# Context keys for two batches at once, first tokens by tiles and new ranks in a planned cross-attention kernel

## The chip, the cores and the metric

The kernel runs on one core of a Trainium2 chip. That core has TensorE (matrix products; PE, with PEld for its weight loads), VectorE (DVE), ScalarE (ACT), GpSimd (POOL) and SyncE (SP, here only a queue that issues DMAs). The metric is the device time of one launch in microseconds (us), as the median of several runs. The profiler records one execution; its span goes from the first to the last instruction.

## The reference, cut to what matters

Two layers over 16 batches of 256 tokens with 256 features, and a context of 77 tokens a batch. All data is float32.

```python
# layer 0
h = rmsnorm(x, sa_norm_w);   h = x + attention(h, h, sa_wq, sa_wk, sa_wv, sa_wo)    # 16 heads of 16
hn = rmsnorm(h, ca_norm_w);  h = h + attention(hn, context, ca_wq, ca_wk, ca_wv, ca_wo)
hn = rmsnorm(h, mlp_norm_w); h = h + (silu(hn @ w_gate) * (hn @ w_up)) @ w_down      # 1024 wide
# layer 1, with layer 0's output as queries and the context as features
norm_X, norm_F = layernorm(context), layernorm(h)
attended = softmax(norm_F @ norm_X.T / 16) @ norm_X                                  # one head of 256
cross = gelu(attended @ fc1_w.T + fc1_b) @ fc2_w.T + fc2_b                           # through 4 features
n = layernorm(cross);  own = softmax(n @ n.T / 16) @ n
out = norm_F + gamma2 * (cross + gamma1 * own)
```

`attention` takes scores of each head times 1/4, a softmax over the keys, the weighted values and the output matrix. The context enters layer 0 through `ca_wk` and `ca_wv`, which don't depend on the tokens.

## The kernel before

**Work.** The program takes the batches one by one in layer 0, and in pairs (`UB = 2`) for loading tokens, for storing them and for layer 1 (the last pair in layer 1 batch by batch). Each piece of the work is a Python generator, called a stream. For a batch there are `self_operands` (norm, transposes psq, psk, psv), `self_maxima` (scores `sc`, row maxima by VectorE), `exponentials` (scores again, transposed, as `st`, exponentials by ScalarE into `pT`), `outputs` (`po`, values with a column of ones), `projection` (division and `wo`); the same for the context with a leading `c` (`csc`, `cst`, `cpo`, `cwo`), fed by `cross_queries` (`pscq`) and `cross_keys`; then `mlp` (`pg`, `pu`, `wd`). For a pair there are `second_context` and `second`, which are layer 1.

**Heads.** A head has 16 features, so score products use 32 rows of TensorE at a time and value products 32 columns. A step of the program has a shape: `f` (full array), `r` (row groups) or `c` (column groups). All score products share one set of four PSUM banks (`sc_banks`); one product must be read out before the next can start.

**Context keys.** `cross_keys(b)` transposes the 77 context tokens of a batch (`tpc`, copied to `ctxT`), multiplies them by `cwk` (`psck`), writes the masked keys `ckm` with ScalarE and the keys with ones `ckx` with VectorE, then makes the values (`pscv`, copied into `cvone`). `ckm` and `ckx` have two buffers, one batch each. `load_context` loads one batch ahead of that, into `cx`.

**Order.** Four engines (TensorE, ScalarE, VectorE, GpSimd) run in an order that a planner in the program writes out (class `Order`). Every stream yields steps with a duration, the data it needs, buffers it acquires and releases, and what it gives. At each turn the planner takes the first TensorE step by this key:

```python
wait = 20 if "f" in (self.shape, st.step.shape) else 500
late = t > self.clock["P"] + wait
key = (late, t if late else 0, st.rank)
```

A step counts as late if it could start only more than `wait` ns after TensorE is free; among those not late the lowest rank goes first. Ranks are given with `add(rank, tie, stream)`: about the batch number plus a constant for the stage, from -50 for the context's exponentials to 4 for the MLP, which so fills what is left. SyncE isn't planned by itself: its DMAs go out in the order in which the program writes them, and the queue waits at each for its buffer.

**Start.** SyncE issues the first pair of tokens as one load of 512 KB, then two contexts, the next pair of tokens and the matrices from `cwk` on; ScalarE issues `wq` to `wo`; GpSimd issues three norm weights, makes the identity, and sets constants: `vone` (three buffers of 1024 columns with ones, into which the values are copied), `cvone`, `nmax`. GpSimd also computes the power -1/2 of every norm (`rstd`, line 193).

Of the kernel before, what the change touches and what calls it, by code (L numbers as in the profile page):

```python
# [15 lines left out]
P = 128  # L16
# [13 lines left out]
def kernel(  # L30
# [46 lines left out]
    def tokens(ap, u):  # L77
# [4 lines left out]
        "h": 4, "cx": 2, "cx2": 2, "hn": 3, "hnT_sa": 1, "hnT_ca": 1, "hnT_mlp": 1, "ctxT": 1,  # L82
        "qx": 3, "kx": 3, "vone": 3, "cqT": 2, "cqx": 2, "ckm": 2, "ckx": 2, "cvone": 2, "pT": 2,
        "po": 1,
        "os": 1, "cos": 1, "oq": 1, "coq": 1, "oT": 1, "coT": 1, "sg": 2, "gT": 1,
# [3 lines left out]
    def load_tokens(u):  # L89
        hs[u] = hpool.tile([P, NT, D], F32, tag="h", name=f"h{u}", bufs=BUFS["h"])  # L90
        nc.sync.dma_start(hs[u], tokens(x, u))
# [6 lines left out]
    load_tokens(0)  # L98
    for b in range(2):
        cxs[b] = load_context(b, 1, "cx")  # L100
# [31 lines left out]
    ca_nw = load_columns(ca_norm_w, "ca_nw", nc.gpsimd)  # L132
# [4 lines left out]
    mlp_nw = load_columns(mlp_norm_w, "mlp_nw", nc.gpsimd)  # L137
# [5 lines left out]
    ident = const.tile([P, P], F32, tag="ident", name="ident")  # L143
    make_identity(nc, ident)
# [17 lines left out]

    vones, cvones, maxes = [], [], ([], [])
    for i in range(3):
        t = const.tile([P, QT, NH, 2 * HD], F32, tag=f"vone{i}", name=f"vone{i}")
        nc.gpsimd.memset(t, 1.0)
        vones.append(t)
# [65 lines left out]
    class Order:  # L233
# [72 lines left out]
        def run(self):  # L306
            while self.streams:
                best = None
                aux = []
                for st in self.streams:  # L310
# [3 lines left out]
                    if st.step.pe:  # L314

                        wait = 20 if "f" in (self.shape, st.step.shape) else 500
# [109 lines left out]
    class Attention:  # L426
# [14 lines left out]
        def tile(self, tag, shape, n=""):  # L441
            tag = self.name + tag
            return pool.tile(shape, F32, tag=tag, name=f"{tag}{self.b}_{n}", bufs=BUFS[tag])
# [615 lines left out]
    def context_loads():  # L1059
        for b in range(B):  # L1060
# [3 lines left out]
            if b > 1:  # L1064
                cxs[b] = load_context(b, 1, "cx")
# [76 lines left out]
```

## Time and profile before

| | us |
|---|---|
| median of 3 runs | 1022.9 |
| lowest and highest run | 1022.3, 1024.54 |
| the profiled execution | 1023.16 |
| its span | 1021.4 |
| TensorE busy | 973.7 |
| VectorE busy | 592.5 |
| ScalarE busy | 512.3 |
| GpSimd busy | 85.0 |

The mean granted clock of TensorE is 0.987. The execution's own time is 1.8 us longer than its span: what lies before the first and after the last recorded instruction. Busy times of engines overlap. In a row of the timeline the first number is when the instruction started, the second how long it took; matmul ends are modelled, so distances between starts are the safer measure. Every float32 product shows as two instructions.

### The profile page before, as it was taken

The page shows a single profiled execution, that of the slowest core. Times are in us where ns is not written, and L with a number is a line of the kernel's source. Part 1 is how long each engine was busy: PE and PEld are TensorE (multiplying, and loading weights), DVE is VectorE, ACT ScalarE, POOL GpSimd, SP SyncE. Part 2 cuts the span into 40 slices and gives each one's busy share as a digit, 9 for nine tenths or more (in the row PEclk, how much of TensorE's full clock was granted, in tenths as well). Part 3 has the DMA queues.
Part 4 walks back from the last instruction along what each step waited for, and adds up shares of the span by engine and source line. Part 5 has one row for each costly group of instructions (what it writes and reads, how often), then busy time and mean ns, then how long its engine had stood idle before and what let it go on. Part 6 is the DMA issues. An engine that isn't in the chain of part 4 may idle for free.

```text
span 1021.4 us, 18993 instructions
## 1 busy us (share of the span) xinstructions
PE 973.7 (95%) x8179; PEld 709.6 (69%) x8179; DVE 592.5 (58%) x1032; ACT 512.3 (50%) x900; POOL 85.0 (8%) x122
## 2 busy tenths in 40 slices
PE   5888999999999999999999999999999999999995
PEld 4655666767776777768676786767777677776772
DVE  2866475757565667465674665655764655455542
ACT  3555736443756347363663526555274537343532
POOL 3100000000100001000110001000010002001110
PEclk9999999999999999999999999999999999999995
DMA  9100000000001000000001000010000000000000
GB/s 300 24 9 1 4 1 2 2 1 1 4 8 46 1 1 1 31 25 1 1 7 49 2 1 1 11 46 1 1 1 10 25 2 1 21 1 1 1 22 21
DMA packets 16908, 17.58 MB, mean 17 GB/s; under 512 B 2392, under 2 KB 16312, under 8 KB 16824
## 3 DMA queue, kind: packets, MB, share of 16 engines
q1 hardware_dynamic: 15640, 15.32, 4.7%
q8 instruction: 64, 1.05, 0.4%
q10 hardware_dynamic: 1088, 1.05, 0.3%
q0 software_dynamic: 96, 0.00, 0.1%
q14 instruction: 20, 0.16, 0.1%
HBM read 12.13 MB, written 4.19 MB: 16 GB/s over the span
## 4 chain that ended last, share of the span: by engine, by line
PE 84%; DVE 6%; ACT 5%; DMA 3%; issue 1%; POOL 0%; POOLq 0%; ACTq 0%
PE wd L728 11%; PE pg L699 11%; PE pu L699 10%; PE st L525 7%; PE sc L473 6%; PE po L556 5%; PE cpo L556 3%; PE cst L525 3%; PE psq L399 3%; PE cwo L594 3%; PE pscq L399 3%; PE wo L594 3%; PE psk L399 3%; ACT pT L533 2%; PE psv L626 2%; DMA h<-in_x_dram 2%
## 5 line engine op out<-in xcount | busy, mean ns | idle before, releaser
L533 ACT ACTIVATE pT<-st 128x2048 f32<-128x2048 f32 x64 | 120.4, 1881 | 83.2 <-PE st L525 83.0
L478 DVE TENSOR_REDUCE nmax<-sc 128x8 f32<-128x2048 f32 x64 | 146.4, 2287 | 19.4 <-PE sc L473 18.2
L699 PE MATMUL pg<-hnT_mlp,wg 128*128 128x256 f32 x512 | 129.1, 387 | 0.0
L728 PE MATMUL wd<-wd,gT 128*128 128x256 f32 x512 | 127.5, 388 | 0.0
L699 PE MATMUL pu<-hnT_mlp,wu 128*128 128x256 f32 x512 | 126.9, 385 | 0.5 <-DVE sg L710 0.5
L699 PEld LDWEIGHTS pg<-hnT_mlp,wg 128*128 128x128 f32 x512 | 93.2, 190 | 23.6 <-issue 13.0
L699 PEld LDWEIGHTS pu<-hnT_mlp,wu 128*128 128x128 f32 x512 | 93.4, 190 | 19.0 <-issue 7.4
L728 PEld LDWEIGHTS wd<-wd,gT 128*128 128x128 f32 x512 | 91.9, 190 | 20.5 <-issue 10.0
L710 DVE SCALAR_TENSOR_TENSOR sg<-sg,pg 128x512 f32<-128x512 f32 x64 | 44.0, 688 | 75.3 <-ACT sg L709 75.0
L709 ACT ACTIVATE sg<-pg 128x512 f32<-128x512 f32 x64 | 38.0, 594 | 65.4 <-PE pg L699 65.0
L533 ACT ACTIVATE cpT<-cst 77x2048 f32<-77x2048 f32 x32 | 59.9, 1873 | 19.1 <-PE cst L525 18.8
L556 PE MATMUL po<-pT,vone 128*32 128x256 f32 x1024 | 66.7, 384 | 0.0
L503 DVE TENSOR_REDUCE nmax<-csc 128x16 f32<-128x1232 f32 x32 | 46.1, 1441 | 29.9 <-PE csc L496 29.8
L711 DVE SCALAR_TENSOR_TENSOR gT<-sg,pu 128x512 f32<-128x512 f32 x64 | 43.8, 685 | 25.0 <-PE pu L699 24.1
L556 PEld LDWEIGHTS po<-pT,vone 128*32 128x32 f32 x1024 | 27.6, 109 | 29.2 <-issue 16.0
L193 POOL TENSOR_TENSOR rstd_n<-ve_n,neg_half 128x4 f32<-128x4 f32 (+2 forms) x26 | 22.3, 864 | 248.7 <-DVE ve_n L191 131.7
L399 PE MATMUL pscq<-hnT_ca,cwq 128*128 128x256 f32 x128 | 31.6, 390 | 3.8 <-ACT hnT_ca L359 3.8
L399 PE MATMUL psq<-hnT_sa,wq 128*128 128x256 f32 x128 | 34.3, 407 | 0.6 <-ACT hnT_sa L359 0.6
L556 PE MATMUL cpo<-cpT,cvone 77*32 77x256 f32 x512 | 34.3, 385 | 0.1
L399 PE MATMUL psk<-hnT_sa,wk 128*128 128x256 f32 x128 | 33.9, 397 | 0.0
L626 PE MATMUL psv<-wv,hnT_sa 128*128 128x256 f32 x128 | 31.9, 386 | 0.0
L399 PEld LDWEIGHTS pscq<-hnT_ca,cwq 128*128 128x128 f32 x128 | 23.1, 190 | 10.6 <-ACT hnT_ca L359 4.3
(619 smaller groups left out, 1568.2 us busy)
## 6 DMA issues: line engine op xcount, KB each, us to landing
h<-in_x_dram SPq DMA_DIRECT2D x8, 512.0 KB
out_dram<-h SPq DMA_DIRECT2D x7, 512.0 KB
cx<-in_ctx_dram SPq DMA_DIRECT2D x16, 77.0 KB
cx<-in_ctx_dram SPq DMA_DIRECT2D x8, 154.0 KB
wg<-in_L_xattn_w_gate_dram SPq DMA_DIRECT2D x1, 1024.0 KB
wu<-in_L_xattn_w_up_dram SPq DMA_DIRECT2D x1, 1024.0 KB
wd<-in_L_xattn_w_down_dram SPq DMA_DIRECT2D x1, 1024.0 KB
out_dram<-h SPq DMA_DIRECT2D x2, 256.0 KB
```

The costliest lines, as they stand in the source:

```text
L399: nc.tensor.matmul(ps[:, m * n : (m + 1) * n], lhsT=w[:, c, m * P : (m + 1) * P], rhs=srcT[:, c, :], start=(c == 0), stop=(c == NC - 1),)
L473: nc.tensor.matmul(sc[:, j, (1 - e) * S : (2 - e) * S], lhsT=a.qx[rg, c, e, qt * P : (qt + 1) * P], rhs=a.kx[rg, c, e], start=True, stop=True,
L478: nc.vector.tensor_reduce(maxima_of(nm, qt)[:, :, c::NC], sc.rearrange("p j (y k) -> p j y k", y=2), AX.X, ALU.max, negate=True,)
L503: nc.vector.tensor_reduce(maxima_of(nm, qt), sc[:, :, : 2 * NC * SK].rearrange("p j (n k) -> p j n k", k=SK), AX.X, ALU.max, negate=True,)
L525: nc.tensor.matmul(st[:nk, j, e * S : (e + 1) * S], lhsT=a.kx[rg, c, e, kc * P : kc * P + nk], rhs=a.qx[rg, c, e], start=True, stop=True,)
L533: nc.scalar.activation(a.pT[k][:nk].rearrange("p j e q -> p j (e q)"), st[:nk], AF.Exp, scale=HD ** -0.5,)
L556: nc.tensor.matmul(po[RG * j : RG * (j + 1), e, :], lhsT=a.v[:nk, kc, 8 * c + 2 * j + e, :], rhs=pT[:nk, j, e, :], start=(first and e == 0 ...
L594: nc.tensor.matmul(ps[:, i * D : (i + 1) * D], lhsT=oT[:, c, i * P : (i + 1) * P], rhs=a.w[:, c, :], start=(c == 0), stop=(c == NC - 1),)
L626: nc.tensor.matmul(ps[:, t * D : (t + 1) * D], lhsT=hnT[:, c, t * P : (t + 1) * P], rhs=wv[:, c, :], start=(c == 0), stop=(c == NC - 1),)
L699: nc.tensor.matmul(ps[:, i * S : (i + 1) * S], lhsT=w[:, c, (f + i) * P : (f + i + 1) * P], rhs=hnT[:, c, :], start=(c == 0), stop=(c == N ...
L710: nc.vector.scalar_tensor_tensor(sg, sg, 1.0, ps, ALU.add, ALU.mult)
L728: nc.tensor.matmul(ps[:, :D], lhsT=gT[:, f, i * P : (i + 1) * P], rhs=wd[:, f, :], start=(f == 0), stop=(f == NF - 1),)
```

## The change

- `cross_keys` takes a pair of batches: four transposes into one bank, one copy to `ctxT` (154 columns), one `psck` of 154 columns, one `ckm` and one `ckx` for both; values still by batch. `ckm`, `ckx` and `cx` have one buffer, which holds a pair. They are released by the pair's last batch. Contexts are loaded by pairs.
- The first pair of tokens is loaded as four tiles of 128 tokens, with the first pair of contexts after two of them.
- The `vone` memsets move from GpSimd to VectorE; the identity is made first on GpSimd; `ca_nw` and `mlp_nw` are loaded from SyncE's queue.
- `os`, `oq` and `oT` are shared by self and cross attention; `os` has two buffers.
- `wait` between row and column steps is 100 ns in place of 500. `cross_maxima` needs the batch before it (`cmT`, b - 1) in place of the one before that.
- Ranks come from a table with a constant for every stage, one added for the first two batches and one for the last three.
- Planned time to landing of context loads is 4000 ns in place of 3000.

```diff
-        "h": 4, "cx": 2, "cx2": 2, "hn": 3, "hnT_sa": 1, "hnT_ca": 1, "hnT_mlp": 1, "ctxT": 1,
-        "qx": 3, "kx": 3, "vone": 3, "cqT": 2, "cqx": 2, "ckm": 2, "ckx": 2, "cvone": 2, "pT": 2,
+        "h": 4, "cx": 1, "cx2": 2, "hn": 3, "hnT_sa": 1, "hnT_ca": 1, "hnT_mlp": 1, "ctxT": 1,
+        "qx": 3, "kx": 3, "vone": 3, "cqT": 2, "cqx": 2, "ckm": 1, "ckx": 1, "cvone": 2, "pT": 2,
         "po": 1,
-        "os": 1, "cos": 1, "oq": 1, "coq": 1, "oT": 1, "coT": 1, "sg": 2, "gT": 1,
+        "os": 2, "oq": 1, "oT": 1, "sg": 2, "gT": 1,
...
-    def load_tokens(u):
-        hs[u] = hpool.tile([P, NT, D], F32, tag="h", name=f"h{u}", bufs=BUFS["h"])
-        nc.sync.dma_start(hs[u], tokens(x, u))
+    def load_tokens(u, t=None):
+
+        if not t:
+            hs[u] = hpool.tile([P, NT, D], F32, tag="h", name=f"h{u}", bufs=BUFS["h"])
+        part = slice(NT) if t is None else slice(t, t + 1)
+        nc.sync.dma_start(hs[u][:, part], tokens(x, u)[:, part])
...
-    load_tokens(0)
-    for b in range(2):
-        cxs[b] = load_context(b, 1, "cx")
+    for t in range(NT):
+        if t == QT:
+            cxs[0] = load_context(0, UB, "cx")
+        load_tokens(0, t)
...
+    ident = const.tile([P, P], F32, tag="ident", name="ident")
+    make_identity(nc, ident)
     sa_nw = load_columns(sa_norm_w, "sa_nw", nc.gpsimd)
+
+    vones, cvones, maxes = [], [], ([], [])
+    for i in range(3):
+        t = const.tile([P, QT, NH, 2 * HD], F32, tag=f"vone{i}", name=f"vone{i}")
+        nc.vector.memset(t, 1.0)
+        vones.append(t)
...
-    ca_nw = load_columns(ca_norm_w, "ca_nw", nc.gpsimd)
+    ca_nw = load_columns(ca_norm_w, "ca_nw", nc.sync)
...
-    mlp_nw = load_columns(mlp_norm_w, "mlp_nw", nc.gpsimd)
+    mlp_nw = load_columns(mlp_norm_w, "mlp_nw", nc.sync)
...
-    ident = const.tile([P, P], F32, tag="ident", name="ident")
-    make_identity(nc, ident)
...
-    vones, cvones, maxes = [], [], ([], [])
-    for i in range(3):
-        t = const.tile([P, QT, NH, 2 * HD], F32, tag=f"vone{i}", name=f"vone{i}")
-        nc.gpsimd.memset(t, 1.0)
-        vones.append(t)
...
-                        wait = 20 if "f" in (self.shape, st.step.shape) else 500
+                        wait = 20 if "f" in (self.shape, st.step.shape) else 100
...
-            tag = self.name + tag
-            return pool.tile(shape, F32, tag=tag, name=f"{tag}{self.b}_{n}", bufs=BUFS[tag])
+        def tile(self, tag, shape, n="", shared=False):
+            tag = tag if shared else self.name + tag
+            return pool.tile(shape, F32, tag=tag, name=f"{self.name}{tag}{self.b}_{n}", bufs=BUFS[tag])
...
+    def last_of_pair(a):
+        return a.b % UB == UB - 1
+
     def cross_maxima(a):
         for qt in range(QT):
             yield Step(
                 T_CS, "r", "sc", ops=[("V", 1440)], free=True,
-                needs=[a.key("q"), a.key("k")] + [("cmT", a.b - 2)] * (a.b > 1),
-                rel=[("cqT", a.b), ("ckm", a.b)] * (qt == QT - 1),
+                needs=[a.key("q"), a.key("k")] + [("cmT", a.b - 1)] * (a.b > 0),
+                rel=([("cqT", a.b)] + [("ckm", a.b // UB)] * last_of_pair(a)) * (qt == QT - 1),
...
-            rel = [(a.name + t, a.b) for t in ("qx", "kx")]
+            rel = [(a.name + "qx", a.b)]
+            if not a.name:
+                rel.append(("kx", b))
+            elif last_of_pair(a):
+                rel.append(("ckx", b // UB))
...
-                acq=[("po",)] * first + [(tag("os"), a.b)] * (end and c == 0),
+                acq=[("po",)] * first + [("os", n, a.b)] * (end and c == 0),
...
-                    a.os = a.tile("os", [P, 2, NC, S])
+                    a.os = a.tile("os", [P, 2, NC, S], shared=True)
...
-        oq = a.tile("oq", [P, NC * S // RG, 2, HD])
+        oq = a.tile("oq", [P, NC * S // RG, 2, HD], shared=True)
...
-        oT = a.tile("oT", [P, NC, S])
+        yield Step(ops=[("V", 690)], acq=[("oT", n, a.b)], rel=[("oq", n, a.b)])
+        oT = a.tile("oT", [P, NC, S], shared=True)
...
-    def cross_keys(a):
-        b = a.b
-        yield Step(NC * 71, ops=[("A", 285)], needs=[("cx", b)] + [("cv", b - 1)] * (b > 0), acq=[("ctxT", b)], rel=[("cx", b)])
-        cx = cxs.pop(b)[:, 0, :]
-        tp = mm_bank(f"tpc{b}")
+    def cross_keys(pair):
+
+        a = pair[0]
+        u = a.b // UB
+        yield Step(NC * UB * 71, ops=[("A", 400)], needs=[("cx", u)], acq=[("ctxT", u)], rel=[("cx", u)])
+        cx = cxs.pop(u)
+        tp = mm_bank(f"tpc{u}")
         for c in range(NC):
-            nc.tensor.transpose(
-                tp[:, c * SK : (c + 1) * SK], cx[:, c * P : (c + 1) * P], ident[:SK, :SK]
-            )
-        ctxT = pool.tile([P, NC, SK], F32, tag="ctxT", name=f"ctxT{b}", bufs=1)
-        nc.scalar.copy(ctxT.rearrange("p c k -> p (c k)"), tp[:, : NC * SK])
-        yield Step(4 * 224, ops=[("A", 390)] * 2 + [("V", 350)] * 4, needs=["cwk"],
-                   acq=[("ckm", b), ("ckx", b)], gives=[a.key("k")])
-        ps = yield from project_T(cwk, ctxT, f"psck{b}")
-        a.k = a.tile("km", [P, NC, 2, SK])
-        masked(a.k[:, :, 1], a.k[:, :, 0], ps)
-        a.kx = a.tile("kx", [P, NC, 2, SK])
-        with_ones(a.kx, ps)
-        yield Step(2 * T_MM, ops=[("A", 390)], needs=["cwv"], acq=[("cvone", b)], rel=[("ctxT", b)],
-                   gives=[a.key("v")], free=True)
-        cv = cvones[b % 2]
-        ps = mm_bank(f"pscv{b}")
-        for c in range(NC):
-            nc.tensor.matmul(
-                ps[:SK, :D], lhsT=ctxT[:, c, :], rhs=cwv[:, c, :],
-                start=(c == 0), stop=(c == NC - 1),
-            )
-        nc.scalar.copy(cv[:, :, :HD], ps[:SK, :D].rearrange("p (n d) -> p n d", d=HD))
-        a.v = cv.unsqueeze(1)
+            for i in range(UB):
+                n = c * UB + i
+                nc.tensor.transpose(
+                    tp[:, n * SK : (n + 1) * SK], cx[:, i, c * P : (c + 1) * P], ident[:SK, :SK]
+                )
+        ctxT = pool.tile([P, NC, UB * SK], F32, tag="ctxT", name=f"ctxT{u}", bufs=1)
+        nc.scalar.copy(ctxT.rearrange("p c k -> p (c k)"), tp[:, : NC * UB * SK])
+        yield Step(4 * 264, ops=[("A", 530)] * 2 + [("V", 440)] * 4, needs=["cwk"],
+                   acq=[("ckm", u), ("ckx", u)], gives=[t.key("k") for t in pair])
+        ps = yield from project_T(cwk, ctxT, f"psck{u}")
+        km = a.tile("km", [P, NC, 2, UB * SK])
+        masked(km[:, :, 1], km[:, :, 0], ps)
+        kx = a.tile("kx", [P, NC, 2, UB * SK])
+        with_ones(kx, ps)
+        for i, a in enumerate(pair):
+            ks = slice(i * SK, (i + 1) * SK)
+            a.k, a.kx = km[:, :, :, ks], kx[:, :, :, ks]
+            yield Step(2 * T_MM, ops=[("A", 390)], needs=["cwv"], acq=[("cvone", a.b)],
+                       rel=[("ctxT", u)] * (i == UB - 1), gives=[a.key("v")], free=True)
+            cv = cvones[a.b % 2]
+            ps = mm_bank(f"pscv{a.b}")
+            for c in range(NC):
+                nc.tensor.matmul(
+                    ps[:SK, :D], lhsT=ctxT[:, c, ks], rhs=cwv[:, c, :],
+                    start=(c == 0), stop=(c == NC - 1),
+                )
+            nc.scalar.copy(cv[:, :, :HD], ps[:SK, :D].rearrange("p (n d) -> p n d", d=HD))
+            a.v = cv.unsqueeze(1)
...
-        for b in range(B):
+        for u in range(NU):
             yield Step(
-                ops=[("S", 100)], acq=[("cx", b)], gives=[("cx", b)], lag=3000 if b > 1 else 6000
-            )
-            if b > 1:
-                cxs[b] = load_context(b, 1, "cx")
+                ops=[("S", 100)], acq=[("cx", u)], gives=[("cx", u)], lag=4000 if u else 6000
+            )
+            if u:
+                cxs[u] = load_context(UB * u, UB, "cx")
...
-            yield Step(ops=[("S", 100)], acq=[("cx2", u)], gives=[("cx2", u)], lag=3000)
+            yield Step(ops=[("S", 100)], acq=[("cx2", u)], gives=[("cx2", u)], lag=4000)
...
-    add = lambda rank, b, gen: order.streams.append(Stream((rank, b), gen))
-    add(-3, 0, loads())
-    add(-3, 1, context_loads())
-    add(-3, 2, second_loads())
-    add(1, 3, second_constants())
-    first = -50
+
+
+    RANKS = {
+        "loads": (-3, 0, 0),
+        "second_constants": (1, 50, 0),
+        "outputs": (1.5, 0, 0),
+        "exponentials": (-1.5, 0, 0),
+        "projection": (1.25, 0, 0),
+        "cross_outputs": (3, 0, 0),
+        "cross_exponentials": (-50, 0, 0),
+        "cross_projection": (-50, 0, 0),
+        "self_maxima": (-1, 0, -50),
+        "cross_maxima": (-49, 0, 0),
+        "cross_queries": (1.75, 0, -1),
+        "self_operands": (-1.5, 0, 1.5),
+        "cross_keys": (2, 0, 0),
+        "mlp": (4.25, 0.25, -1),
+        "second_context": (4, 0, -50),
+        "second": (1, 0, 0),
+    }
+
+    def add(stage, b, tie, gen):
+        always, early, late = RANKS[stage]
+        rank = b + always + (early if b < 2 else 0) + (late if b >= B - 3 else 0)
+        order.streams.append(Stream((rank, tie), gen))
...
     for b in range(B):
-        a, ca = Attention(b, "", S, wo), Attention(b, "c", SK, cwo)
-        add(b + 1, 0, outputs(a))
-        add(b - 1.5, 1, exponentials(a))
-        add(b + 1, 2, projection(a))
-        add(b, 0, outputs(ca))
-        add(b + first, 1, exponentials(ca))
-        add(b + first, 2, projection(ca))
-        add(b - 0.75, 1, self_maxima(a))
-        add(b + 1, 1, cross_maxima(ca))
-        add(b + 2, 3, cross_queries(ca))
-        add(b - 1.5, 5, self_operands(a))
-        add(b + 2, 5, cross_keys(ca))
-        add(b + 4, 4, mlp(b))
+        a, ca = Attention(b, "", S, wo), crosses[b]
+        add("outputs", b, 0, outputs(a))
+        add("exponentials", b, 1, exponentials(a))
+        add("projection", b, 2, projection(a))
+        add("cross_outputs", b, 0, outputs(ca))
+        add("cross_exponentials", b, 1, exponentials(ca))
+        add("cross_projection", b, 2, projection(ca))
+        add("self_maxima", b, 1, self_maxima(a))
+        add("cross_maxima", b, 1, cross_maxima(ca))
+        add("cross_queries", b, 3, cross_queries(ca))
+        add("self_operands", b, 5, self_operands(a))
+        if b % UB == 0:
+            add("cross_keys", b, 5, cross_keys(crosses[b : b + UB]))
+        add("mlp", b, 4, mlp(b))
     for u in range(NU):
-        add(UB * u + 1, 3, second_context(u))
+        add("second_context", UB * u, 3, second_context(u))
 
         for first in range(0, UB, UB if u < NU - 1 else 1):
             nb = UB if u < NU - 1 else 1
-            add(UB * u + first + 1, 2, second(u + first, u, first, nb))
+            add("second", UB * u + first, 2, second(u + first, u, first, nb))
```

The table `RANKS` (constant, added for the first two batches, added for the last three) against the constants before:

| stage | before | after |
|---|---|---|
| outputs | 1 | 1.5 |
| exponentials | -1.5 | -1.5 |
| projection | 1 | 1.25 |
| cross_outputs | 0 | 3 |
| cross_exponentials, cross_projection | -50 | -50 |
| self_maxima | -0.75 | -1, last three -50 more |
| cross_maxima | 1 | -49 |
| cross_queries | 2 | 1.75, last three -1 more |
| self_operands | -1.5 | -1.5, last three +1.5 more |
| cross_keys | 2 | 2 (first batch of the pair) |
| mlp | 4 | 4.25, first two +0.25, last three -1 more |
| second_context | 1 | 4, last three -50 more |
| second | 1 | 1 |
| second_constants | 1 | 51 |

More of the change, by code (lines that the diff above doesn't have):

```diff
@@ L439, in key @@
             return (self.name + what, self.b, *more)
-        def tile(self, tag, shape, n=""):
-            tag = self.name + tag
-            return pool.tile(shape, F32, tag=tag, name=f"{tag}{self.b}_{n}", bufs=BUFS[tag])
+        def tile(self, tag, shape, n="", shared=False):
+            tag = tag if shared else self.name + tag
+            return pool.tile(shape, F32, tag=tag, name=f"{self.name}{tag}{self.b}_{n}", bufs=BUFS[tag])
     def maxima_rows(a, nm):
@@ L538, in outputs @@
     def outputs(a):
-        n, tag = a.name, lambda t: a.name + t
+        n = a.name
         for k, (c, kc, nk) in enumerate(a.steps):
@@ L562, in outputs @@
                 if c == 0:
-                    a.os = a.tile("os", [P, 2, NC, S])
+                    a.os = a.tile("os", [P, 2, NC, S], shared=True)
                 nc.vector.transpose(a.os[:, :, c], po)
     def projection(a):
-        n, tag = a.name, lambda t: a.name + t
+        n = a.name
         yield Step(
             ops=[("V", 360), ("V", 690, 1)], needs=[a.key("os", c) for c in range(NC)],
-            acq=[(tag("oq"), a.b)], rel=[(tag("os"), a.b)],
+            acq=[("oq", n, a.b)], rel=[("os", n, a.b)],
         )
@@ L582, in projection @@
         )
-        yield Step(ops=[("V", 690)], acq=[(tag("oT"), a.b)], rel=[(tag("oq"), a.b)])
-        oT = a.tile("oT", [P, NC, S])
+        yield Step(ops=[("V", 690)], acq=[("oT", n, a.b)], rel=[("oq", n, a.b)])
+        oT = a.tile("oT", [P, NC, S], shared=True)
         nc.vector.transpose(
@@ L587, in projection @@
         )
-        steps = in_halves(ops=[("V", 690)], rel=[(tag("oT"), a.b)], gives=[a.key("h")])
+        steps = in_halves(ops=[("V", 690)], rel=[("oT", n, a.b)], gives=[a.key("h")])
         for i in range(QT):
@@ new lines, in add @@
+    def add(stage, b, tie, gen):
+        always, early, late = RANKS[stage]
+        rank = b + always + (early if b < 2 else 0) + (late if b >= B - 3 else 0)
+        order.streams.append(Stream((rank, tie), gen))
+    add("loads", 0, 0, loads())
+    add("loads", 0, 1, context_loads())
+    add("loads", 0, 2, second_loads())
+    add("second_constants", 0, 3, second_constants())
+    crosses = [Attention(b, "c", SK, cwo) for b in range(B)]
+    for b in range(B):
+        a, ca = Attention(b, "", S, wo), crosses[b]
[12 more added lines that the diff above has]
+        add("mlp", b, 4, mlp(b))
```

## The prediction

> **What bounds the kernel now.** I read the page first, then a table by stage (40 windows of the span), then the timeline of the first 16 us, then TensorE's timeline over one period of the steady part. The page:
>
> ```profile
> span 1021.4 us, 18993 instructions
> ...
> PE 973.7 (95%) x8179; PEld 709.6 (69%) x8179; DVE 592.5 (58%) x1032; ACT 512.3 (50%) x900; POOL 85.0 (8%) x122
> ...
> PE   5888999999999999999999999999999999999995
> ...
> PEclk9999999999999999999999999999999999999995
> ```
>
> TensorE is busy for 973.7 of 1021.4 us at full clock, except at both ends. So there are only two ways to gain: take work off TensorE, or fill its 47.7 us of idle time. The stage table says where that idle time lies; the columns are stretch, length, then busy time of PE, PEld, DVE, ACT, POOL:
>
> ```profile
> 0.00:25.50 25.50, 15.08 (x74) 11.63 (x74) 7.60 (x17) 9.65 (x24) 9.43 (x22) 1.00 0.95 300
> 25.50:51.10 25.60, 22.25 (x201) 16.30 (x200) 20.88 (x31) 13.23 (x29) 3.12 (x13) 1.00 0.12 24
> 51.10:76.60 25.50, 21.30 (x224) 14.77 (x224) 17.86 (x35) 13.62 (x24) 2.13 (x4) 1.00 0.03 9
> 76.60:102.10 25.50, 21.97 (x236) 14.35 (x236) 15.71 (x21) 14.20 (x23) 1.34 (x2) 1.00 0.01 1
> ...
> 587.30:612.80 25.50, 25.50 (x170) 20.80 (x169) 16.38 (x27) 7.13 (x16) 0.70 (x1) 1.00 0.00 1
> ...
> 663.90:689.40 25.50, 24.20 (x240) 16.99 (x229) 14.31 (x22) 14.25 (x31) 2.09 (x3) 1.00 0.13 46
> ...
> 995.90:1021.40 25.50, 13.25 (x51) 7.24 (x50) 5.80 (x23) 6.85 (x15) 1.96 (x2) 0.50 0.06 21
> ```
>
> Length minus PE busy: 10.4 us in the first window; 12.7 us from 25.5 to 128 us (the three rows shown, 3.4, 4.2 and 3.5, and two smaller ones); about 6 us in the seven hundred microseconds of the steady part, nearly all of it in stretches like 663.9:689.4 (1.3 us, once a pair of batches); about 6 us from 868 to 996; 12.3 us in the last window, where the clock has fallen to half and one dependent chain runs. In the steady part pscq starts at 438.50, 559.30 and 680.16 us: a pair of batches takes 120.8 us, almost all of it TensorE work.
>
> The start (columns: start, duration, engine):
>
> ```profile
> 5.62 0.42 ACT L341 ACTIVATE sq_sa<-h 128x256 f32<-128x256 f32 x1 [1.46 <-DMA h<-in_x_dram]
> ...
> 6.70 2.17 DVE L191 TENSOR_SCALAR ve_sa<-ss_sa 128x2 f32<-128x2 f32 x1 [6.70 <-ACT sq_sa L341]
> ...
> 7.76 1.08 POOL L174 MEMSET nmax<- 128x256 f32 x4
> ...
> 9.03 0.73 POOL L193 TENSOR_TENSOR rstd_sa<-ve_sa,neg_half 128x2 f32<-128x2 f32 x1 [0.18 <-DVE lone L158]
> ...
> 9.79 0.91 ACT L347 ACTIVATE hn_sa<-h,rstd_sa 128x256 f32<-128x256 f32 x2 [2.95 <-POOL rstd_sa L193]
> ...
> 12.21 3.78 PE L399 MATMUL psq<-hnT_sa,wq 128*128 128x256 f32 x8 [0.56 <-ACT hnT_sa L359]
> ```
>
> The first square waits for the 512 KB token load, landed at 5.6. Then ve_sa, a 128x2 operation that takes 0.17 us at 13.49, takes 2.17. Its end (8.87) and that of POOL's last memset (7.76 + 1.08 = 8.84) fall together. The power rstd_sa is queued on POOL behind these memsets, so 9.03 would stand even if ve_sa had been quick. Everything up to psq hangs on it.
>
> One place in the steady part:
>
> ```profile
> 590.74 1.89 PE L699 MATMUL pg<-hnT_mlp,wg 128*128 128x256 f32 x8
> 592.47 1.89 PE L699 MATMUL pu<-hnT_mlp,wu 128*128 128x256 f32 x8
> 594.19 1.01 PE L399 MATMUL psck<-ctxT,cwk 128*128 128x77 f32 x8
> 595.04 1.03 PE L656 MATMUL pscv<-cwv,ctxT 128*77 128x256 f32 x4
> ```
>
> Start to start, the eight key matmul instructions of 77 columns cost 595.04 - 594.19 = 0.85 us, 106 ns each.
>
> **The change part by part.**
>
> *Keys of two batches at once.* TensorE: 2 x 0.85 = 1.70 us a pair becomes eight instructions of 154 columns. The rows of 256 columns (pg, 592.47 - 590.74) cost 1.73/8 = 216 ns, 0.84 ns a column, so 77 columns would be 65 ns by columns and are 106: something that doesn't shrink with the columns sets them. At 154 columns I take 0.84 x 154 = 130 ns, 1.04 us in all: 0.66 us saved a pair. [...] Seven pairs lie in stretches where TensorE is saturated: 7 x 0.66 = 4.6 us. Transposes (4 a pair), values pscv (8) and their copies stay as many.
>
> ACT and DVE get less too: the four ckx pieces took 1.15 us (287 ns each), kx pieces of 256 took 475, so 154 columns are about 370 and a pair saves 2.30 - 1.47 = 0.8 us of DVE. It counts only once. From 31.6 to 37.6 us the chain of waits runs through the second batch's own keys: ctxT, psck (after 0.73 us idle), ckm, 1.15 us of ckx, then nmax. With its keys made with those of batch 0 this piece goes; DVE still has some of it earlier. I take 1.0 us (bounds 0 and 1.9).
>
> *Single buffers of ckm and ckx.* A new wait: the next pair's keys wait for the last cst of this pair. The tightest gap before is from cst ending at 570.8 to csc at 597.7: 27 us for a piece of some 4 us (1.0 matmul, two masks, 1.5 DVE). MLP matmuls cover it: zero. Without that cover it would be 4 us a boundary.
>
> *Tokens by tiles.* Two tiles (256 KB) are needed instead of four. 512 KB took 4.84 us from issue; a row of half this size under this load doesn't exist. Bounds: no gain, and 1.46 us (ACT's table load ends at 4.16). I take 1.0, landing at 4.6. SP issues three more tile loads and ca_nw, mlp_nw, one context load fewer: at 0.4 us each its issue of cwk comes by about 3.7; before it stood at 5.03, with a hole from 2.5. No cost. On POOL, sa_nw is issued behind the identity, perhaps 0.5 us later; it landed 5.8 us after issue, and hnT_sa needs it at 8.6 in the new time. Slack of 1 us: zero, at worst 1.
>
> *Value constants on DVE.* POOL loses three 1024-column memsets (2.8 us) and two DMA issues (0.73, 0.72), so its queue ends near 4.5 and rstd_sa no longer waits. DVE, idle until 6.7, gets three memsets: from 165 ns for 128 columns and 1.05 ns a column (the slope of ckx to kx) about 1.1 us each, 3.3 in all. Whether they run beside POOL's remaining memsets is not in the trace; the nearest row is the stalled ve_sa. Read as "DVE stands while POOL sets memory", both together end near 6.7 and ve_sa waits a microsecond. [...]
>
> Start in sum: tokens at 4.6, squares to 5.7, ve_sa 5.9, rstd_sa to 6.7, hn_sa at 6.7 against 9.79: 3.1 us (1 to 3.5).
>
> *Ranks, wait of 100 ns, os/oq/oT shared.* The order of all instructions on four queues changes, and no row shows the new one. Unchanged for sure: matmul work, the single set of score banks, four h buffers. So the 1.3 us a pair, where ACT stands at sq_sa for the x load with hnT_ca queued behind it, may stay. cross_maxima at the top, and cross_queries earlier, bring mlp(0), the first filler, forward: pscq of batch 0 ended about 90.0, its csc came at 93.9 and 96.7. second_constants (rank 51) leaves the chain at 50 to 58 us for idle slots, and mlp(0), which needs its gT, comes 80 us later. At the end, the last self_maxima early and mlp ranked ahead can fill part of the 6 us. I take 2 us of the 12.7 and 1.5 of the 6: 3.5 us, an estimate; bounds +8 (more turns, below) and -15 (most of 12.7 and 6 filled). The shared oq and oT add waits on DVE, where reductions are queued behind; the planner leaves room: zero, at worst one wo (1.9 us) a batch where TensorE has no other work. The last window's chain stays.
>
> Sum: 4.6 + 1.0 + 3.1 + 3.5 = 12.2 us. The profiled execution took 1023.16; the median of the runs is 0.26 lower. 1023.2 - 12.2 - 0.3 = **1010.7 us**, said as 1011. Some 0.2% (2 us) is what the measurement can tell from no change.
>
> **The rivals.**
>
> *More turns: slower.* Between 559 and 680 us the 40 steps on row or column groups stand in 29 blocks; some run straight on (sc then po, cst then cpo). A block costs: the matmuls after it 1.93 instead of 1.73 (0.20), the half before it 0.95 instead of 0.86 (0.09), so 0.29 us. cpo, now ranked behind cross_queries and self_operands, no longer follows cst at once, and at 100 ns fewer steps are waited for. If all 40 stood alone: 11 x 0.29 x 8 = 25 us, 1036. It decides from 12.2/(8 x 0.29) = 5 more blocks a pair; 7 more, which I take for this case, give 1011 + 16 = 1027. For: wait and rank both point there. Against: cpo then may join sc or st instead.
>
> *The order is worth much more.* Most of the early idle and of 868 to 996 us filled, and two blocks a pair fewer (4.6 us): 1011 - 9 - 5 = about 998 to 1003.
>
> *The start is eaten.* From 25 to 115 us the single score bank set with DVE and ACT sets the pace, and the new order loses there what the start gives; or memsets and sa_nw take 2 us of it. Only the keys' 4.6 us are left: 1018.
>
> *Pairing doesn't save TensorE time* (spacing proportional to columns after all): 1016.
>
> **How the numbers follow.** Main case, 1005 to 1015: 0.56. Order worth more, under 1005: 0.18. Start eaten or no saving in pairing, 1015 to 1021: 0.12, faster. No change within 2 us: 0.05. More turns, over 1025: 0.09. Faster 0.86, same 0.05, slower 0.09. Range 1000 to 1020: it leaves out about 0.06 below and 0.14 above.
>
> **What would show it.** psck: 64 instructions at some 130 ns spacing. hn_sa first at 6.5 to 7.0, POOL free before ve_sa. A period of pscq near 120.2 us if the order is neutral; lower means fewer blocks, over 121 the first rival. TensorE's idle below 11 us from 25 to 128. Wrong: hn_sa after 8.5, psck at 200 ns, or a period over 122.

## The result, and the profile after

| | before | after |
|---|---|---|
| median of 6 runs each, us | 1023.72 | 1017.48 |
| lowest and highest run | 1022.3, 1025.83 | 1016.74, 1017.89 |
| the profiled execution | 1023.16 | 1016.78 |

The ratio of the runs is 0.9936, interval 0.9922 to 0.9951: 6.2 us less by the medians, 6.4 by the profiled executions. The forecast was 12 us less. The page of the kernel after:

```profile
span 1015.0 us, 18822 instructions
...
PE 971.6 (96%) x8115; PEld 702.6 (69%) x8115; DVE 587.8 (58%) x1003; ACT 509.1 (50%) x876; POOL 80.7 (8%) x117
...
PE   6888899999999999999999999999999999999995
...
PEclk9999999999999999999999999999999999999995
```

TensorE is busy 2.1 us less (971.6 against 973.7), and idle 4.3 us less (43.4 against 47.7). The keys alone should have taken 5 us from the busy time. Something gave more than half of that back, and the digits of PEclk, in tenths, don't show it. The stage table does (stretch, length, busy time of PE, PEld, DVE, ACT, POOL, granted clock, DMA share, GB/s):

```profile
0.00:25.50 25.50, 16.84 (x92) 12.81 (x92) 9.32 (x21) 12.16 (x31) 5.95 (x18) 1.00 0.97 297
25.50:51.10 25.60, 22.16 (x224) 15.76 (x224) 18.76 (x31) 14.97 (x28) 3.11 (x13) 1.00 0.15 32
51.10:76.60 25.50, 21.57 (x204) 13.91 (x196) 17.21 (x29) 10.51 (x18) 2.07 (x3) 0.93 0.00 1
76.60:102.10 25.50, 22.55 (x215) 14.54 (x212) 13.60 (x16) 14.21 (x24) 0.00 (x0) 0.93 0.02 7
...
587.30:612.80 25.50, 25.50 (x228) 17.68 (x226) 13.33 (x21) 8.80 (x11) 0.70 (x1) 1.00 0.00 1
...
663.90:689.40 25.50, 25.50 (x227) 18.18 (x220) 13.54 (x19) 11.87 (x22) 0.00 (x0) 1.00 0.13 42
```

From 51 to 102 us the clock is 0.93, where it was 1.00 before. Four narrower windows of the same kernel place it, each pair a stretch in which TensorE has little to do and the one behind it:

```profile
70.00:72.00 2.00, 0.20 (x4) 0.20 (x8) 0.73 (x4) 2.00 (x3) 0.84 (x2) 1.00 0.00 0
72.00:76.00 4.00, 3.87 (x44) 2.02 (x45) 0.17 (x1) 3.32 (x7) 0.69 (x1) 0.61 0.01 4
84.00:86.00 2.00, 0.36 (x8) 0.21 (x7) 0.00 (x0) 1.98 (x2) 0.00 (x0) 1.00 0.12 41
86.00:90.00 4.00, 4.00 (x35) 2.30 (x36) 2.16 (x2) 0.64 (x2) 0.00 (x0) 0.57 0.07 23
```

The start of the kernel after:

```profile
4.32 0.38 ACTq L113 DMA_DIRECT2D wo<-in_L_xattn_sa_wo_dram  x1
...
4.72 1.28 ACT L345 ACT_TABLE_LOAD   x1 [4.72 <-DMA wq<-in_L_xattn_sa_wq_dram]
...
6.02 0.42 ACT L345 ACTIVATE sq_sa<-h 128x256 f32<-128x256 f32 x1
...
7.10 0.17 DVE L195 TENSOR_SCALAR ve_sa<-ss_sa 128x2 f32<-128x2 f32 x1 [3.00 <-ACT sq_sa L345]
...
7.43 0.73 POOL L197 TENSOR_TENSOR rstd_sa<-ve_sa,neg_half 128x2 f32<-128x2 f32 x1 [2.88 <-DVE head_mask L161]
...
8.19 0.91 ACT L351 ACTIVATE hn_sa<-h,rstd_sa 128x256 f32<-128x256 f32 x2 [0.82 <-POOL rstd_sa L197]
...
10.62 3.78 PE L403 MATMUL psq<-hnT_sa,wq 128*128 128x256 f32 x8 [0.56 <-ACT hnT_sa L363]
```

POOL no longer holds rstd_sa back, ve_sa takes 0.17 us, and psq starts at 10.62 in place of 12.21. But the first square starts at 6.02, not before, because ScalarE's table load stands until 4.72, where it started at 2.88. The keys, in a place with full-array work on both sides:

```profile
728.64 1.22 PE L403 MATMUL psck<-ctxT,cwk 128*128 128x154 f32 x8
729.69 1.89 PE L674 MATMUL pscv<-cwv,ctxT 128*77 128x256 f32 x8
```

729.69 - 728.64 = 1.05 us for a pair, 131 ns an instruction, where two batches took 1.70.

### The profile page after: what moved, and what is told of

It reads as the page before. It is cut to its first block, busy times and chain, and to the rows that moved or that the text cites. A ratio compares the mean times of both kernels' runs of the same rounds, so it can differ in the third digit from the quotient of the medians.

```text
span 1015.0 us, 18822 instructions
## 1 busy us (share of the span) xinstructions
PE 971.6 (96%) x8115; PEld 702.6 (69%) x8115; DVE 587.8 (58%) x1003; ACT 509.1 (50%) x876; POOL 80.7 (8%) x117
## 3 DMA queue, kind: packets, MB, share of 16 engines
q8 instruction: 64, 1.05, 0.4%
q10 hardware_dynamic: 1088, 1.05, 0.3%
## 4 chain that ended last, share of the span: by engine, by line
PE 83%; DVE 8%; ACT 5%; DMA 3%; issue 1%; POOL 0%; ACTq 0%; POOLq 0%; SPq 0%
PE wd L746 11%; PE pu L717 10%; PE pg L717 10%; PE st L536 6%; PE sc L477 6%; PE po L567 5%; PE cst L536 3%; PE cwo L605 3%; PE psq L403 3%; PE cpo L567 3%; PE wo L605 3%; DVE nmax L482 2%; PE psv L637 2%; PE psk L403 2%; ACT pT L544 2%; PE pscq L403 2%
## 5 line engine op out<-in xcount | busy, mean ns | idle before, releaser
L751 DVE TENSOR_TENSOR h<-h,wd 128x256 f32<-128x256 f32 x32 | 13.3, 417 | 50.7 <-PE wd L746 50.6
L197 POOL TENSOR_TENSOR rstd_ca<-ve_ca,neg_half 128x2 f32<-128x2 f32 x16 | 11.1, 694 | 263.2 <-DVE ve_ca L195 263.2
```

## The experiments

The theory that these profiles suggest (A): keys and start are paid out as the traces show them, 5.3 and 1.6 us, and the new order gives nothing in sum. Each ratio below is to the kernel before, run beside it.

### The start alone

```diff
 # before, with the start of after; contexts still one by one
-    load_tokens(0)
-    for b in range(2):
-        cxs[b] = load_context(b, 1, "cx")
+    for t in range(NT):
+        if t == QT:
+            for b in range(2):
+                cxs[b] = load_context(b, 1, "cx")
+        load_tokens(0, t)
...
-        nc.gpsimd.memset(t, 1.0)
+        nc.vector.memset(t, 1.0)
```

> The kernel before with the changed start alone: first tokens as four tiles, identity first, value constants set by VectorE, two norm weights loaded from SyncE's queue; contexts still one by one, so the written order of the four engines stays that of before. Theory A (the start is paid out to the end): the profile after has psq at 10.62 us against 12.21, so 1.6 us less, 1022.1 if before is at 1023.7, and psq at about 10.6. Rival (the early stage, paced by score banks, DVE and ACT, eats it): psq as early, time as before within 0.5 us.

1022.27 us, ratio 0.9992 (0.9983 to 1.0001). The span of the profiled execution is 1.6 us shorter (1019.8), as theory A has it; psq starts at 10.55. The runs show 0.8 us with an interval that reaches both answers. They scatter with the granted clock, so runs of the same mean clock say more: at 0.988 they took 1021.60 us (median of 11) against 1022.49 (19 runs of before), at 0.985 1023.16 (6) against 1024.67 (10). That is 0.9 and 1.5 us less: a part of the 1.6 arrives, at least; whether all of it does stays open.

### First tokens in halves

```diff
 # after
-    for t in range(NT):
-        if t == QT:
-            cxs[0] = load_context(0, UB, "cx")
-        load_tokens(0, t)
+    load_tokens(0, 0)
+    cxs[0] = load_context(0, UB, "cx")
+    load_tokens(0, QT)
```

(`load_tokens` takes two tiles at a time.)

> The changed kernel with the first tokens loaded as two halves of 256 KB in place of four tiles of 128 KB: two DMA issues fewer on SyncE's queue ahead of wo. Theory A (with four tiles, [...]wo, stands in ScalarE's queue until wq has landed, and ScalarE's table load stands behind it, 4.72 us in place of 2.88): table load back at about 2.9, first square at 4.2 to 4.8, psq at 9.0 to 9.4, time 1.3 us below the changed kernel, about 1016. Rival (the token data sets it): first square at 6.0 as in the changed kernel, same time, 1017.5.

1015.53 us, ratio 0.9918 (0.9899 to 0.9937). Its start in the timeline:

```profile
2.31 0.49 ACTq L112 DMA_DIRECT2D wo<-in_L_xattn_sa_wo_dram  x1
...
2.83 1.28 ACT L344 ACT_TABLE_LOAD   x1 [2.83 <-issue]
...
4.38 0.42 ACT L344 ACTIVATE sq_sa<-h 128x256 f32<-128x256 f32 x1 [0.26 <-DMA h<-in_x_dram]
...
6.78 0.91 ACT L350 ACTIVATE hn_sa<-h,rstd_sa 128x256 f32<-128x256 f32 x2
...
9.21 3.78 PE L402 MATMUL psq<-hnT_sa,wq 128*128 128x256 f32 x8 [0.56 <-ACT hnT_sa L362]
```

wo is issued at 2.31 instead of 4.32, the table load follows at once, the square waits for the tokens alone, and hn_sa starts at 6.78. Two loads fewer ahead of wo free ScalarE's queue 2 us earlier: shown. By medians the gain over after is 2 us, 1.4 of it at psq; the ratios' intervals overlap (after: 0.9922 to 0.9951). The profiled execution is the fastest of the six, with 1013.36 us and a mean clock of 0.988; from 25.5 to 128 us its clock is 1.00. The other five took 1014.96 to 1016.32 us at 0.983 to 0.985. So the same kernel lost clock in most executions and not in this one; the section on the half clock says why.

### Wait of 500 ns

```diff
 # after
-                        wait = 20 if "f" in (self.shape, st.step.shape) else 100
+                        wait = 20 if "f" in (self.shape, st.step.shape) else 500
```

> The changed kernel with the wait between row and column steps at 500 ns in place of 100; ranks as changed. Theory A (the short wait splits blocks: 241 in the profile after against 229 before, 0.29 us each): blocks at about 230, time 3 us below the changed kernel, 1014.5. Rival (the split comes from the ranks, the wait does little or keeps TensorE idle): blocks at 240 and 1017 to 1019.

1024.24 us, ratio 1.0001 (0.9991 to 1.0011): theory A falls in the form that blames the short wait for the blocks. The long wait costs the changed kernel 7 us, and it makes more blocks, 246 against 241 (before: 229), not fewer. TensorE is busy 977.7 us, 6.1 more than in after, and the clock from 25.5 to 128 us is 0.93. An estimate parts the 6.1: this execution has 17.07 us at half clock ahead of the low stretch at its end, where after has 6.83. That is 0.5 x 10.24 = 5.1 us of work at most, and five blocks at 0.29 are 1.5. A block here is a run of row or column steps between full-array steps, counted on TensorE's timeline.

### Old ranks, keys alone, ranks alone

Three kernels part the keys from the order. The first is after with the old ranks and 500 ns (`cross_maxima` still needs the batch just before it, as in after):

```diff
 # after; RANKS filled with the constants of before
-        "cross_maxima": (-49, 0, 0),
+        "cross_maxima": (1, 0, 0),
...
-        "mlp": (4.25, 0.25, -1),
+        "mlp": (4, 0, 0),
```

> The changed kernel with the ranks of before and the wait of 500 ns; keys by pairs, start and shared tiles stay. Theory A (keys and start alone make the gain, and the new order gave about nothing in sum): 5.3 us of psck and 1.6 us of start less, about 1017 where the changed kernel has 1017.5. Rival (the new order brought a gain of its own, as forecast with 3.5 us): 1020 to 1021. If the old ranks are better for this kernel: under 1015.

The second is before with the paired `cross_keys`, its loads and its releases (to make room, one small tile has one buffer in place of two):

```diff
-        "h": 4, "cx": 2, "cx2": 2,
+        "h": 4, "cx": 1, "cx2": 2,
...
-        add(b + 2, 5, cross_keys(ca))
+        if b % UB == 0:
+            add(b + 2, 5, cross_keys(crosses[b : b + UB]))
```

> The kernel before with the keys by pairs alone (one buffer of ckm and ckx for a pair, contexts loaded by pairs); start, ranks, wait and separate os, oq, oT as before; a small constant tile has one buffer in place of two to make room. Theory B (the loss of the changed kernel under the old ranks, 1038.9, comes from the single pair buffer: the next pair's keys wait for the last cst of this pair, and the low ranks of the context stages leave TensorE without work): 1034 to 1040, TensorE idle over 55 us. Rival C (it comes from the shared os, oq and oT): keys give their 5.3 us, about 1018.

The third is before with the table of ranks and 100 ns (`cross_maxima` needs the batch two back, as in before):

```diff
-    add = lambda rank, b, gen: order.streams.append(Stream((rank, b), gen))
+    def add(stage, b, tie, gen):
+        always, early, late = RANKS[stage]
...
+        add("cross_keys", b, 5, cross_keys(ca))
```

> The kernel before with the new ranks and the wait of 100 ns, and nothing else: keys by batch with two buffers each. Theory D (the new ranks mainly repair what pairing costs): 1021 to 1026. Rival E (the new order is worth much by itself, here too): 1005 to 1016, which would make the pairing a loss.

| | keys by batch | keys by pairs |
|---|---|---|
| old ranks, 500 ns | 1022.6 to 1023.7 (before) | 1038.93, ratio 1.0149 (1.013 to 1.0168) |
| new ranks, 100 ns | 1034.6, ratio 1.0112 (1.0088 to 1.0137) | 1017.48 (after) |

Old ranks on the changed kernel gave 1038.86, ratio 1.0158 (1.0134 to 1.0183). So each half of the change alone costs 12 to 16 us, and together (with the start and the shared tiles) they gain 6. Neither theory A nor the forecast (gains that add) allows that. The stage table of the keys alone:

```profile
25.50:128.00 102.50, 86.57 (x824) 56.50 (x825) 60.39 (x91) 54.28 (x92) 7.79 (x21) 0.92 0.05 11
128.00:868.00 740.00, 725.61 (x6264) 523.95 (x6261) 441.82 (x701) 369.83 (x614) 49.84 (x60) 1.00 0.03 10
```

TensorE's idle time rises from 47.7 to 1037.6 - 977.2 = 60.4 us, and the clock from 25.5 to 128 us is 0.92. A mean of 0.92 there means up to 8% of the window's work not done: 0.08 x 102.5 = 8 us. Two more stretches of 3.41 us at half clock, from 288.06 and 465.56 us, vanish in the 1.00 of the second row; with them it is 12 us at most. That fits TensorE's busy time, which rises by 3.5 us although the psck take 5.7 less and the blocks fall to 219. So the loss shows as idle time and as low clock, not as more turns. The ranks alone keep the clock at 1.00 from 25.5 to 128 us, and idle time rises by only 3 us. TensorE is busy for 983.7 us, 10 more than before: 251 blocks, 22 more, are 6.4 us at 0.29, and 10.2 us at half clock, from 157.81 and 758.56 us on, are 5.1 at most.

### Shared tiles alone

```diff
 # before
-        "os": 1, "cos": 1, "oq": 1, "coq": 1, "oT": 1, "coT": 1, "sg": 2, "gT": 1,
+        "os": 2, "oq": 1, "oT": 1, "sg": 2, "gT": 1,
```

> The kernel before with os (two buffers), oq and oT shared by self and cross attention, and nothing else. Theory B (pair buffers): 1022 to 1025, as before. Rival C (sharing makes VectorE stand with reductions queued behind): 1030 or more, TensorE idle over 55 us.

1021.38 us, ratio 0.9989 (0.9982 to 0.9996). Rival C falls: sharing costs nothing.

### The rank of cross_maxima

```diff
 # after
-        "cross_maxima": (-49, 0, 0),
+        "cross_maxima": (1, 0, 0),
```

> The changed kernel with the rank of cross_maxima back at 1 in place of -49. Theory B (with one pair buffer the context scores must go as soon as they can, so that the buffer comes free): slower than the changed kernel by 8 us or more, 1026 to 1036. Rival (this rank matters no more than any other): 1014 to 1021.

1022.78 us, ratio 1.0 (0.999 to 1.001): 5 us slower than after, between the two expectations. Without this one rank the whole gain over before is gone: 253 blocks in place of 241, TensorE busy for 975.3 us in place of 971.6.

### A second pair buffer

```diff
 # before with keys by pairs and shared os, oq, oT
-        "ckm": 1, "ckx": 1,
+        "ckm": 2, "ckx": 2,
```

(To make room, `fc1_sb` lies in a working tile.)

> The kernel before with keys by pairs and two pair buffers each of ckm and ckx (room made by sharing os, oq and oT, which alone cost nothing, and by placing one small weight in a working tile); ranks, wait and start as before. Theory B (the single pair buffer makes the loss of the keys alone, 1038.9): with the second buffer the keys give their 5.3 us, 1016 to 1019, TensorE idle near 44 us. Theory F (the buffer is not the cause; keys that come once a pair simply land badly in an order tuned for keys by batch): 1030 to 1040 as with one buffer.

1034.09 us, ratio 1.012 (1.0103 to 1.0137), where one buffer gave 1.0149 (1.013 to 1.0168). The second buffer gives back 5 of the 16 us by the medians, 3 by the ratios, whose intervals overlap, and the shared tiles alone were good for 1.2; theory B falls for the rest. The same edit on after with halves:

> The changed kernel with tokens in halves (1015.5) and two pair buffers each of ckm and ckx. Theory B: a wait is taken away, 1010 to 1015. Theory F (any edit shuffles the order, and these ranks fit one buffer only): 1016 to 1035.

1024.21 us, ratio 1.0009 (1.0 to 1.0018): a wait taken away, and 9 us slower. This is what theory F expects: ranks that fit one set of buffers lose by an edit that moves the planner's order. Which waits the new order adds was not traced.

### The half clock

Two gaps on TensorE stand before the two stretches of low clock of the kernel after (the number in brackets is the idle time before the instruction):

```profile
71.80 1.15 PE L536 MATMUL st<-qx__298,kx__319 32*128 32x256 f32 x16 [2.00 <-ACT pT L544]
...
85.95 0.88 PE L503 MATMUL csc<-cckm__250,ccqT__798 32*128 32x154 f32 x16 [1.64 <-ACT pT L544]
```

The next kernel fills them with work that nobody reads:

```diff
 # after, in exponentials, behind the st matmuls
+            if not a.name and b == 1 and k in (0, 3):
+                busy = mm_bank(f"busy{k}")
+                for i in range(14):
+                    nc.tensor.transpose(busy[:, i % 4 * P : (i % 4 + 1) * P], ident, ident)
```

> The changed kernel with 14 transposes of the identity into an unused bank after each of two st steps of batch 1 (k = 0 and k = 3, at 68.7 and 82.8 us in the profile after), where TensorE stood idle for 2 us each and the granted clock then fell to half for some 3.4 us twice; their output is not used. Theory G (the half clock is set off by these gaps and costs the changed kernel what it shows): granted clock 1.00 from 25.5 to 128 us in place of 0.97, time 2 to 3 us below the changed kernel, 1014.5 to 1015.5. Rival (the slow matmuls lie beside waits for ScalarE and VectorE anyway, or the clock falls elsewhere): 1017 to 1018, or the clock still 0.95 to 0.98.

1013.77 us, ratio 0.9902 (0.9885 to 0.9918), clear of after's 0.9922 to 0.9951: 28 useless transposes make the program 3.5 us faster. Its windows, over the same stretches as the four of after:

```profile
70.00:72.00 2.00, 2.00 (x26) 1.65 (x27) 1.72 (x8) 0.95 (x1) 0.79 (x2) 1.00 0.03 8
72.00:76.00 4.00, 2.81 (x39) 1.57 (x36) 0.33 (x2) 3.63 (x7) 1.29 (x2) 1.00 0.00 0
84.00:86.00 2.00, 2.00 (x23) 1.67 (x19) 0.00 (x0) 1.59 (x2) 0.00 (x0) 1.00 0.00 0
86.00:90.00 4.00, 3.89 (x57) 2.46 (x55) 2.06 (x2) 1.26 (x3) 0.00 (x0) 1.00 0.12 39
```

The clock stays at 1.00, in this window and from 25.5 to 128 us as a whole. The planner doesn't count the transposes, so the order of all other work is that of after. The gain is a little over the 2 to 3 us expected. That the low clock costs what it shows, and that filling the gaps removes it, is shown.

That the gaps by themselves set it off, the other half of theory G, is not so. After with halves has the same two gaps, and its profiled execution kept its clock:

```profile
71.22 1.15 PE L535 MATMUL st<-qx__296,kx__317 32*128 32x256 f32 x16 [2.00 <-ACT pT L543]
...
84.70 0.81 PE L502 MATMUL csc<-cckm__248,ccqT__796 32*128 32x154 f32 x16 [1.64 <-ACT pT L543]
```

What differs is how the gaps lie on a grid of time. In the traces every stretch of low clock, but for the one at the end, takes 3.41, 6.83 or 10.24 us, whole multiples of 3.41, and those of one execution start whole multiples of 3.41 us apart (after: 72.91 and 86.57, 4 x 3.41). From execution to execution the grid is shifted. Here are pieces of it in the kernel after:

```profile
69.50:72.91 3.41, 1.41 (x28) 0.76 (x21) 1.36 (x7) 2.78 (x5) 1.34 (x2) 1.00 0.00 0
72.91:76.32 3.41, 3.28 (x32) 1.78 (x32) 0.00 (x0) 2.67 (x3) 0.69 (x1) 0.50 0.02 5
...
83.16:86.57 3.41, 1.77 (x36) 1.23 (x28) 0.00 (x0) 3.00 (x4) 0.00 (x0) 1.00 0.13 46
86.57:89.98 3.41, 3.41 (x27) 1.77 (x20) 2.16 (x2) 0.07 (x1) 0.00 (x0) 0.50 0.02 5
```

And in after with halves, where the grid follows from the low clock at the end, which starts at 987.92 us:

```profile
66.33:69.74 3.41, 2.09 (x21) 1.20 (x19) 3.34 (x8) 0.45 (x1) 0.69 (x1) 1.00 0.00 0
69.74:73.15 3.41, 1.93 (x32) 1.14 (x32) 0.61 (x4) 3.05 (x6) 1.38 (x2) 1.00 0.02 5
...
83.39:86.80 3.41, 2.10 (x34) 1.32 (x35) 1.22 (x1) 2.00 (x3) 0.00 (x0) 1.00 0.20 51
```

Ahead of each fall TensorE is busy for 1.41 and 1.77 of 3.41 us, 41 and 52%. Each gap lies within one piece. With halves a line cuts each gap in two, at 69.74 and at 83.39, and no piece is under 56%. Over all fourteen traces, from about 18 to 980 us and without pieces already at half clock, half clock followed 16 of 18 pieces in which TensorE was busy for less than 50%, 7 of 28 with 50 to 60%, and 1 of 3867 above. So gaps of 2.00 and 1.64 us cost 0.5 x 3.41 = 1.7 us of TensorE work each in the execution of after and nothing in that of halves, and in the traces the two differ by where the grid lies; two such falls are the 3.4 us that the transposes gave back.

### A warm start

```diff
 # after with halves
+    warm = mm_bank("warm")
+    for i in range(20):
+        nc.tensor.transpose(warm[:, i % 4 * P : (i % 4 + 1) * P], ident, ident)
     order = Order({**BUFS, "pair": 1})
```

> The changed kernel with tokens in halves and 20 transposes of the identity into an unused bank ahead of everything on TensorE, from about 2.6 us on; their output is not used. If the first psq (3.8 us for what later takes 1.7) and psk (2.2 to 2.7) are slow because the clock is still at half, they take 1.8 each and the time falls by 2 to 2.6 us, 1013 to 1013.5. Rival (they are slow for weights that land late, or the early stage eats it): psq stays over 3 us or the time stays at 1015.5.

1013.39 us, ratio 0.991 (0.9895 to 0.9925). Against halves alone that is 2.1 us less by the medians, as expected, but 0.8 by the ratios (0.9918, 0.9899 to 0.9937), whose intervals overlap: the gain is not settled. Behind the transposes the first products are fast all the same:

```profile
2.64 4.53 PE L1091 MATMUL warm<-ident 128*128 128x128 f32 x20 [2.64 <-POOL neg_half L155]
...
6.96 0.72 PE L653 MATMUL tpc<-ident,cx 77*128 77x77 f32 x4
...
8.04 0.91 ACT L350 ACTIVATE hn_sa<-h,rstd_sa 128x256 f32<-128x256 f32 x2
...
10.11 1.99 PE L402 MATMUL psq<-hnT_sa,wq 128*128 128x256 f32 x8 [0.56 <-ACT hnT_sa L362]
...
11.94 1.89 PE L402 MATMUL psk<-hnT_sa,wk 128*128 128x256 f32 x8
...
13.66 1.67 PE L636 MATMUL psv<-wv,hnT_sa 128*128 128x256 f32 x7
```

psq and psk take 1.83 and 1.72 us, start to start. Late weights were not what made them slow elsewhere: with the gaps filled but no warm start, psq begins later than here, at 11.56 for 10.11 us, and is slow.

```profile
11.56 3.78 PE L403 MATMUL psq<-hnT_sa,wq 128*128 128x256 f32 x8 [0.56 <-ACT hnT_sa L363]
```

The pace of TensorE was. Instruction by instruction, the spacing goes from 427 to 216 ns in the middle of psk, at about 17.88 us in before, 14.88 in after, 15.13 with halves and 16.29 with the gaps filled, and each of these times is a line of that execution's grid (72.91 - 17 x 3.413 = 14.89). The clock column reads 1.00 there all the same, but the traces of before and after hold a record of the clock only from these times on, 17.87 and 14.89 us. That the start ran at half clock is thus an inference from the factor of two in the spacing, not a reading of the clock. The 20 transposes have their price: tpc starts at 6.96 us, with halves alone at 5.69, hn_sa (8.04) waits behind ctxT (7.72) in ScalarE's queue, and psq starts 0.9 us later than with halves alone. From 25.5 to 128 us this execution then has a clock of 0.95, where the profiled one of halves alone had 1.00.

## Why the prediction was right, and by which steps

**Direction and range** held: 1017.5 in 1000 to 1020. The size did not: 6 us, where 12 were forecast. The time lies outside the main case and next to the rival "the start is eaten" (1018), which had the place right: from 25.5 to 128 us the new kernel lost about what its start and its end won. A part of the loss was half clock, which the rival doesn't name. That the sum still fell into the range was in part luck, since it put the cost of single buffers at zero and had no term for what the two halves of the change cost each other's order: alone each loses 12 to 16 us.

- *Keys: 4.6 us of TensorE.* Right. 1.05 us a pair against 1.04 forecast; summed start to start over all psck, 14.6 us become 9.3. The spacing is not proportional to the columns: 106 ns an instruction at 77 columns, 131 at 154. What holds 77 columns at 106 ns no run shows.
- *Start: 3.1 us.* Mis-sized: 1.6 at psq. The term "tokens land at 4.6, squares to 5.7" failed. SP's extra issues were counted for SP's own queue ("no cost"), not for ScalarE's, whose fourth load and table load stood behind them (4.32 and 4.72 us, before 2.35 and 2.88). SP's own queue was late too: cwk went out at 5.56, not by 3.7. With halves hn_sa starts at 6.78, the 6.7 of the forecast. Memsets on VectorE cost nothing, as the author's estimate of 3.1 us assumed: 0.91 us each, between 1.04 and 4.1, beside POOL's own, which take what they took before (cvone 0.99 us both times, nmax 1.06 for 1.08).
- *Single pair buffers: zero, covered by MLP matmuls.* Wrong as a statement about the keys by themselves (16 us slower under the old ranks, 12.7 us more idle time on TensorE), and hidden in the sum because the ranks came with them. The buffer itself is only part of it: a second one returns 3 to 5 of the 16.
- *Order: 3.5 us from fuller ends.* Right for the end, wrong for the early stage. Before and after:

```profile
25.50:128.00 102.50, 90.69 (x941) 61.47 (x940) 65.83 (x105) 61.17 (x107) 8.03 (x21) 1.00 0.04 10
868.00:1021.40 153.40, 135.03 (x861) 101.93 (x859) 70.72 (x173) 59.60 (x114) 12.85 (x14) 0.91 0.03 11
```

```profile
25.50:128.00 102.50, 88.95 (x864) 59.07 (x861) 65.95 (x97) 55.64 (x94) 7.30 (x20) 0.97 0.05 10
868.00:1015.00 147.00, 131.23 (x841) 98.98 (x839) 64.82 (x167) 58.33 (x111) 13.54 (x16) 0.92 0.03 12
```

TensorE's idle time from 868 us on falls from 18.4 to 15.8 us, more than the 1.5 forecast. From 25.5 to 128 us, where 2 us were to be won, it rises from 11.8 to 13.6, and the half clock takes up to 3.4 us there; filling the two gaps gave 3.5. (The forecast's 12.7 us of idle time reach to 153 us; up to 128 they are 11.8.) If the terms added, 5.3 and 1.6 of the 6.2 measured would leave 0.7 us lost by the order.
- *Rival "more turns".* The place was right: 241 blocks for 229, 12 x 0.29 = 3.5 us by the forecast's own price. Of its two reasons the wait was wrong: with the new ranks 100 ns makes fewer blocks than 500. The ranks do make more: 251 against 229 with the keys by batch (the wait changed with them).
- *Early keys: 1.0 us.* Not separated by any run.
- *The signs.* psck came at 131 ns. hn_sa came at 8.19, between the sign of being right (6.5 to 7.0) and that of being wrong (8.5). Idle time from 25 to 128 us went up and not below 11. The period of pscq can't be read in the new order: two batches lie between 98 us (625.46 to 723.52) and 125 us (441.12 to 566.35) apart.

What stays open: how the 16 us of the keys alone divide. Up to 12 us of work lost to the clock, 3 to 5 for the buffer and 12.7 of idle time overlap, because slow work can run where TensorE would have waited. Why the new ranks lose with keys by batch and pay with keys by pairs is argued from the blocks and the clock; no run follows a single wait through. The changed need of `cross_maxima` was not tested alone.

## What to carry to other kernels

An order tuned by ranks is part of the data layout: change what is made together and its ranks have to be chosen anew, and neither half can be judged alone. Forecast such a pair as one edit with wide bounds, not as two savings that add. And where TensorE is thinly filled, look at the granted clock behind it: here a gap of 2.00 us cost another 1.7 us after it had ended, in one execution and not in another. So don't compare two kernels by one profiled execution each without comparing their clocks.

## What the runs showed of the hardware

The clock fell to half for 3.41 us at a time, in the execution of after behind pieces of 3.41 us in which TensorE was busy for 41 and 52%. Gaps of 2.00 and 1.64 us were enough there and not in the execution of after with halves, and before the change a gap of 2.44 us ahead of 73.5 us did no harm: a line of its grid, 72.48, cuts it in two, and TensorE was busy for 57 and 71% of the pieces on its two sides. The grid of 3.41 us is shifted from execution to execution. That the place of a gap on it decides fits the traces; no order was traced with two positions of the grid.

And loads issued from SyncE's queue can hold up one in ScalarE's: wo went out at 4.32 us, and at 2.31 with two loads fewer on SyncE's. The profile names the landing of wq as what released the table load behind it, at 4.72 us; by what the queue was held no run shows.
